# Cross-attention with LayerNorm: a new order for the last ten tiles, gamma and beta in two PSUM banks, late moments partly on ScalarE

## The chip, the cores and the metric

The kernel runs on one core of a Trainium2 chip. The core has five engines that run side by side, each through its own instructions in the order in which they were written: TensorE (PE: matrix products; PEld is its weight load), VectorE (DVE), ScalarE (ACT), GpSimd (POOL) and SyncE (SP, which only issues transfers). ACT and POOL issue transfers too. Matrix products are written to PSUM, eight banks of 128 partitions by 512 fp32 numbers; everything else lies in SBUF. The metric is the time of one execution on the device in microseconds (us); lower is better. A profile covers one execution; its span runs from the first instruction to the last.

## The reference

```python
qs = (q @ wq).reshape(Bq, Lq, H, HD).transpose(0, 2, 1, 3)
ks_ = (k @ wk).reshape(Bq, Lk, H, HD).transpose(0, 2, 1, 3)
vs = (v @ wv).reshape(Bq, Lk, H, HD).transpose(0, 2, 1, 3)
scores = jnp.einsum('bhqd,bhkd->bhqk', qs, ks_) / jnp.sqrt(jnp.float32(HD))
scores = jnp.where(mask[:, None, :, :], -jnp.inf, scores)
attn_w = jax.nn.softmax(scores, axis=-1)
attn = jnp.einsum('bhqk,bhkd->bhqd', attn_w, vs)
attn = attn.transpose(0, 2, 1, 3).reshape(Bq, Lq, H * HD)
out = attn @ wo + q
mu = jnp.mean(out, axis=-1, keepdims=True)
var = jnp.mean((out - mu) ** 2, axis=-1, keepdims=True)
return (out - mu) / jnp.sqrt(var + EPS) * gamma + beta
```

There are 4 batches of 2048 rows of 512 numbers (q), 77 context rows per batch (k and v), 16 heads of 32. In this kernel all is fp32 in and out.

## The kernel before

The 8192 rows are cut into 64 tiles of 128 rows (number t). Two tiles make a pair (b = t // 2). Products that must be exact to fp32 are made from a rounded high part and a low part: each costs three matmuls (high x high, high x low, low x high).

Tiles 0 to 53 are worked off in a loop (lines 600 to 704). For the last ten tiles, 54 to 63, and for the steps of earlier tiles that are still open, the order is written out by hand in the string `ORDER` (lines 45 to 65), and `do` (line 717) calls one step for each word. As each engine runs its instructions as they are written, a word's place settles what it queues behind. The words, by the engine that does them (the number is the tile, or the pair for P, V, a and b; what stands behind the point is a part):

- PE: `S` scores (line 285), four banks; `Q` a projection of queries (line 161); `V` weights x values of a pair (line 383), two banks; `W` the same for one tile, for pair 31 only (line 398), one bank; `O` output projection (line 447), 12 matmuls, one bank; `X` adds the residual on PE by two matmul records of the identity (line 436) ahead of `O`, so that the sum lies in PSUM.
- DVE: `T` masked maxima of four heads (line 299), which also empties a bank of the scores; `r`, `h` reciprocals of the sums (lines 324, 337); `t` transpose of a tile's weights (line 353); `b`, `d` low part of V's or W's product (line 418, written to `AL`); `+` residual for tiles without `X` (line 456); `s` moments by bn_stats and bn_aggr (lines 492 and 494); `y` centre: (out - mean) x gamma (line 518); `z` finish: x 1/std + beta (line 521); `q` copies a query projection.
- ACT: `e` exps of four heads with their sums (line 313); `a`, `c` high part of V's or W's product (line 414, written to `AH`); `k` scale by mean and 1/std (line 509); `K` scale by 1/std (line 512); `i` cast.
- POOL: `n`, `m` normalise the weights (whole tile, line 329; half a tile, line 343); `u` 1/std, two small instructions (lines 499 and 500); `v` the bias for `k`; `f` x gamma, then + beta (lines 483 and 484); `G` + beta (line 515); `j` low part of a cast.
- Transfers: `x` loads rows, `w` stores rows (SP); `P`, `U` move one of twelve parts of the transposed weights of a pair or a tile (line 365); the last letter names the queue: s SP, a ACT, g POOL. The transfer of a part starts when its `t` has run, and `V` or `W` needs all twelve.

So a late tile ends in one of three ways: `y` and `z` on DVE; `y`, `K`, `G`; or `k` and `f`. Row data lie in `od[t]`, in SBUF; while a tile's sum is still in PSUM it stands in `pos[t]`. All banks of PSUM come from one ring (`bank`, line 96): an allocation waits until the last reader of the bank eight allocations earlier is done. `gam` and `bet` are the rows of gamma and beta, spread over the partitions, in SBUF.

The last tiles end in the same order before and after the change: `W62`, `c62` (AH), `d62` (AL), `W63`, `X63`, `c63`, `d63`, `O62`, `O63`, then `s63`, `u63`, `y63`, `z63`, `w63`.

Of the kernel before, what the change touches and what calls it, by code (L numbers as in the profile page):

```python
# [42 lines left out]


ORDER = """
S54 T54.0 Q59 q58 T54.2 x57 i31 T54.3 S55 e54.0 j31 e54.2 T54.1 q59 x61 e54.1 e54.3 t53 T55.0 x52 O49 P26.2a r54
P26.5s T55.1 P26.6s k46 k47 e55.1 T55.2 +49 n54 S56 T55.3 s49 t54 T56.1 e55.2 Q62 q62 O48 T56.0 x56 f47 e55.0 S57
f46 T56.2 +48 e55.3 P26.9g e56.2 Q61 e56.0 r55 s48 T56.3 T57.2 T57.1 n55 T57.0 P26.7g V25 T57.3 S58 e56.3 e56.1 q61
u49 e57.0 P26.3s t55 a25.1 a25.0 P26.4s r56 P26.10s Q63 T58.3 e57.3 P26.8s P26.11s x60 b25.1 e57.2 P27.6g P26.0s w46
T58.0 T58.2 b25.0 q63 n56 x58 P26.1s P27.8s e57.1 P27.5s x62 P27.2g Q60 T58.1 P27.3g v49 e58.2 S59 P27.4g x51 t56  # L50
V26 O50 P27.11g r57 T59.0 P27.7s P27.9g P27.1g T59.2 n57 q60 P27.0g e58.0 P27.10s T59.3 T59.1 w47 t57 e58.1 a26.1
x50 a26.0 e58.3 b26.0 b26.1 e59.0 e59.2 P28.3g S60 P28.7g T60.1 P28.1g r58 u48 O51 T60.0 P28.8s T60.2 e59.1 +50
T60.3 +51 e59.3 n58 x53 t58 e60.3 r59 V27 S61 k49 P28.11s X52 s51 T61.0 T61.2 a27.0 P28.6g P28.10s O53 T61.3 n59 O52
P28.0s P28.2s x54 T61.1 x63 a27.1 e60.2 t59 P28.4g b27.1 e61.1 b27.0 y51 u51 P28.5g e61.2 e61.0 s50 e61.3 x55 f49
P29.2g e60.1 s52 P29.1g x59 S62 P28.9s P29.11s e60.0 T62.3 P29.0g y52 +53 r61 P29.9a T62.1 O55 T62.2 P29.6s T62.0
s53 e62.2 r60 +55 P29.3g u52 P29.5g n61 O54 t61 V28 K51 n60 S63 u53 a28.0 +54 e62.1 b28.0 t60 G51 P30.11g P29.4s
a28.1 P29.10s P29.8s b28.1 e62.0 T63.0 P29.7s P30.0g u50 e62.3 V29 a29.1 a29.0 y48 T63.1 v50 r62 X56 n62 s54 T63.3
w49 b29.1 P30.6g T63.2 b29.0 O57 P30.2s e63.1 P30.4s P30.5s k50 P30.10s t62 P30.9g f50 e63.0 e63.3 h63.0 U62.8g O56
P30.1s O59 y53 P30.8s P30.3s m63.0 e63.2 K53 X58 P30.7s U62.9g V30 U62.3s w50 +57 y54 U62.2s U62.1a U62.0a +59 a30.1
U62.10s s57 h63.1 m63.1 U62.5a s59 u54 O58 U62.4s s56 t63 a30.0 b30.0 K52 w51 U62.11a b30.1 X62 y57 u57 y56 U62.6s  # L60
U63.1g z48 U63.11s O60 G53 U63.7a U63.5g U63.6s O61 s55 U63.9s K54 U63.2g U62.7s U63.0a W62 U63.3s s58 z57 U63.8g
U63.4a +60 G54 c62 G52 U63.10s w53 y58 y59 u59 s60 w57 u56 w52 z59 +61 d62 u58 u60 w48 W63 s61 X63 w54 u55 K56 y55
w59 c63 z58 d63 y61 O62 G56 s62 y60 K55 u61 K60 w58 z61 w56 G55 O63 u62 G60 y62 w55 s63 z62 u63 w61 w60 y63 w62 z63
w63
"""


# [1 line left out]
def xattn_layernorm(  # L69
# [368 lines left out]
    def o_proj(t):  # L438
        b, tt = divmod(t, 2)
        rs = slice(tt * P, tt * P + P)  # L440
        ah, al = at[b]
        first = t not in pos
        if first:
            pos[t] = bank(f"po_{t}")
        for c in range(NC_D):
            for n, (a, w) in enumerate(((ah, woh), (ah, wol), (al, woh))):
                nc.tensor.matmul(  # L447
                    pos[t],
                    a[:, c, rs],
                    w[:, c, :],  # L450
                    start=(first and c == 0 and n == 0),
                    stop=(c == NC_D - 1 and n == 2),
                )

    def residual(t):
        nc.vector.tensor_tensor(od[t], pos.pop(t), od[t], ALU.add)  # L456
# [33 lines left out]
    def moments_one(t):  # L490
# [2 lines left out]
        mvs[t, 1] = sb.tile([P, 4], F32, tag="mvt", bufs=64 - LATE, name=f"mvt_{t}")  # L493
        nc.vector.bn_aggr(mvs[t, 1][:, :2], st)  # L494

    def rsqrt_one(t):
# [2 lines left out]
        nc.gpsimd.tensor_tensor(mv[:, 2:3], mv[:, 1:2], bat[t // TPB][1][:, k : k + 1], ALU.add)
        nc.gpsimd.tensor_tensor(mv[:, 2:3], mv[:, 2:3], mhalf[:, :1], ALU.pow)  # L500
# [10 lines left out]
    def stretch(t):
        nc.scalar.activation(od[t], od[t], AF.Identity, scale=mvs[t, 1][:, 2:3])

# [1 line left out]
        nc.gpsimd.tensor_tensor(od[t], od[t], bet, ALU.add)  # L515

    def centre(t):
        nc.vector.scalar_tensor_tensor(od[t], pos.pop(t, od[t]), mvs[t, 1][:, 0:1], gam, ALU.subtract, ALU.mult)  # L518

    def finish(t):  # L520
        nc.vector.scalar_tensor_tensor(od[t], od[t], mvs[t, 1][:, 2:3], bet, ALU.mult, ALU.add)  # L521
# [273 lines left out]
```

## Time and profile before

| what | us |
|---|---|
| median of 3 runs | 525.09 |
| lowest and highest | 524.68 and 526.96 |
| the profiled execution, its own time | 525.58 |
| its span | 523.8 |
| its time outside of the span | 1.78 |

Times in the rows that follow are counted from the start of the span. The first word of `ORDER`, `S54`, starts on PE at 423.44, so the part of the program that the change touches takes some 100 of the 523.8 us. A row of a timeline gives start, duration, engine, line, operation and shapes, and in square brackets how long the engine had been idle and what ended that. Matmuls overlap: their pace is the distance of two starts, not the duration.

### The profile page before, as it was taken

Reading aid. Unit: us, or ns where it says so; the run is one execution under the profiler, and the core shown is the slowest. Engines: PE = TensorE matmul, PEld = TensorE weight load, DVE = VectorE, ACT = ScalarE, POOL = GpSimd, SP = SyncE. Lnnn points to the kernel's source line nnn. Section 1 sums busy time; section 2 is a strip of 40 time slices with the busy share of each in tenths; the row PEclk is TensorE's granted clock in tenths of the full one; section 3 lists DMA queues with packets and bytes.
Section 4 is the critical chain, followed back from the end, with each engine's and each line's share of the span. In section 5 each row is a group of like instructions: output and inputs, shape, how many; then the busy total and the mean of one; then the engine's idle time right before and its main releaser. Section 6 shows DMA issues by size and latency. Waiting matters only on the chain. (4 is left out here: it accounts for less than half of the span.)

```text
span 523.8 us, 20456 instructions
## 1 busy us (share of the span) xinstructions
PE 511.1 (98%) x6852; PEld 388.8 (74%) x6852; DVE 482.7 (92%) x2584; ACT 467.2 (89%) x2224; POOL 419.8 (80%) x382
## 2 busy tenths in 40 slices
PE   9999999999999999999999999999999999999975
PEld 7977677777777777777777777777777777776653
DVE  5698899899999888999999889989999899999897
ACT  6688899999899999999899999999899999999511
POOL 0635457889799988898799988888989997888885
PEclk9999999999999999999999999999999999999997
DMA  8936667878777978787778788878877878894653
GB/s 309 402 127 163 181 157 200 225 219 239 183 189 211 237 203 229 220 225 197 195 209 233 214 227 215 221 195 225 209 198 209 232 215 191 220 251 133 182 187 140
DMA packets 58584, 110.24 MB, mean 210 GB/s; under 512 B 9392, under 2 KB 11056, under 8 KB 58480
## 3 DMA queue, kind: packets, MB, share of 16 engines
q1 hardware_dynamic: 55264, 102.44, 70.6%
q0 software_dynamic: 2496, 5.77, 4.0%
q8 instruction: 55, 0.90, 0.8%
q10 hardware_dynamic: 720, 0.72, 0.5%
q14 instruction: 49, 0.40, 0.3%
HBM read 41.79 MB, written 16.78 MB: 112 GB/s over the span
## 5 line engine op out<-in xcount | busy, mean ns | idle before, releaser
L313 ACT ACTIVATE pbuf<-pbuf,nm 128x77 f32<-128x77 f32 x1024 | 352.6, 353 | 22.5 <-DVE nm L299 16.6
L313 ACT ACTIVATION_READ_ACCUMULATOR pbuf<-pbuf,nm 128x1 f32 x1024 | 197.6, 193 | 0.0
L299 DVE CUSTOM_DVE_ANT_0 pbuf<-sc,mb 128x77 f32<-128x77 f32 x1024 | 170.5, 230 | 22.9 <-PE sc L285 22.9
L329 POOL TENSOR_TENSOR pbuf<-pbuf,ri 128x1232 f32<-128x1232 f32 x63 | 142.3, 2259 | 29.0 <-DVE ri L324 16.3
L447 PE MATMUL po<-woh,AH 128*128 128x512 f32 x256 | 108.1, 422 | 0.4 <-DVE AL L418 0.4
L447 PE MATMUL po<-woh,AL 128*128 128x512 f32 x256 | 101.4, 396 | 3.6 <-DVE AL L418 3.6
L447 PE MATMUL po<-wol,AH 128*128 128x512 f32 x256 | 101.1, 395 | 0.0
L161 PE MATMUL pq<-xth,wqh 128*128 128x512 f32 (+1 forms) x256 | 98.6, 385 | 0.9 <-DVE nm L299 0.9
L161 PE MATMUL pq<-xtl,wqh 128*128 128x512 f32 (+1 forms) x256 | 97.9, 382 | 0.0
L161 PE MATMUL pq<-xth,wql 128*128 128x512 f32 (+1 forms) x256 | 97.9, 382 | 0.0
L353 DVE STREAM_TRANSPOSE B<-pbuf 128x1280 f32<-128x1280 f32 x64 | 95.4, 1492 | 0.6 <-POOL pbuf L329 0.3
L299 DVE DVE_READ_ACCUMULATOR2_ANT nm<- 128x1 f32 x1024 | 83.2, 81 | 0.0
L483 POOL TENSOR_TENSOR o<-o,gam 128x512 f32<-128x512 f32 x50 | 66.2, 1325 | 13.6 <-ACT o L479 13.6
L285 PEld LDWEIGHTS sc<-kct,q 32*64 32x64 f32 x4096 | 51.3, 130 | 23.8 <-issue 22.8
L484 POOL TENSOR_TENSOR o<-o,bet 128x512 f32<-128x512 f32 x50 | 64.8, 1297 | 3.9
L154 POOL TENSOR_TENSOR xtl<-xtf,xth 128x1024 fp32r<-128x1024 f32 x28 | 67.2, 2401 | 0.0
L285 PE MATMUL sc<-kct,q 32*64 32x77 f32 x4096 | 61.3, 237 | 0.0
L383 PE MATMUL pa<-PT,vsb 96*32 96x256 f32 x992 | 60.0, 382 | 0.5 <-issue 0.3
L447 PEld LDWEIGHTS po<-woh,AH 128*128 128x128 f32 x256 | 48.7, 190 | 15.6 <-issue 1.3
L447 PEld LDWEIGHTS po<-woh,AL 128*128 128x128 f32 x256 | 48.7, 190 | 15.2 <-DVE AL L418 4.5
L161 PEld LDWEIGHTS pq<-xth,wqh 128*128 128x128 f32 x256 | 48.1, 188 | 10.8 <-PE sc L285 1.0
L447 PEld LDWEIGHTS po<-wol,AH 128*128 128x128 f32 x256 | 48.7, 190 | 9.1 <-issue 0.7
(113 smaller groups left out, 681.6 us busy)
## 6 DMA issues: line engine op xcount, KB each, us to landing
PT<-B SPq DMA_DIRECT2D x345, 128.0 KB
xtf<-xT SPq DMA_DIRECT2D x28, 512.0 KB
o<-x SPq DMA_DIRECT2D x56, 256.0 KB
out<-o SPq DMA_DIRECT2D x56, 256.0 KB
PT<-B POOLq DMA_DIRECT2D x25, 128.0 KB, 4.0
o_end<-x SPq DMA_DIRECT2D x8, 256.0 KB
out<-o_end SPq DMA_DIRECT2D x8, 256.0 KB
xtf<-xT SPq DMA_DIRECT2D x4, 256.0 KB
```

The costliest lines, as they stand in the source:

```text
L154: nc.gpsimd.tensor_tensor(l, fx.pop((g, c)), h.bitcast(F32), ALU.subtract)
L161: nc.tensor.matmul(pq, w[:, c, m * P : (m + 1) * P], r[:, c, rs], start=(n == 0), stop=(n == 11))
L285: nc.tensor.matmul(sc[j][half : half + P // 2, g * NK : (g + 1) * NK], qs[q, g, r0 : r0 + P // 2], kct[q, g, t // TPB, keys_of(j)], start= ...
L299: nc.vector.tensor_tensor_reduce(pb[:, h // 2, (h % 2) * NK : (h % 2 + 1) * NK], scs[t][j][:, g * NK : (g + 1) * NK], mb[:, t % TPB, keys_ ...
L313: nc.scalar.activation(pb[:, h // 2, (h % 2) * NK : (h % 2 + 1) * NK], pb[:, h // 2, (h % 2) * NK : (h % 2 + 1) * NK], AF.Exp, bias=nmax[t ...
L329: nc.gpsimd.tensor_tensor(pv, pv, rv.to_broadcast((P, NP, 2, NK)), ALU.mult)
L353: nc.vector.transpose(bt.rearrange("p c q r -> p q c r"), pbuf[t % NPB].rearrange("p q (c r) -> p q c r", c=5),)
L383: nc.tensor.matmul(pas[b, g // 2][HD * j : HD * (j + 1), (g % 2) * BLK : (g % 2 + 1) * BLK], vsb[:, 2 * b // TPB, HD * h : HD * (h + 1)], ...
L447: nc.tensor.matmul(pos[t], a[:, c, rs], w[:, c, :], start=(first and c == 0 and n == 0), stop=(c == NC_D - 1 and n == 2),)
L483: nc.gpsimd.tensor_tensor(o, o, gam, ALU.mult)
L484: nc.gpsimd.tensor_tensor(o, o, bet, ALU.add)
```

## The change

It has five parts.

1. `ORDER` is written anew (396 words for 397). The steps of attention are the same ones. For the ends of the tiles the counts change:

| word | before | after |
|---|---|---|
| s (DVE moments) | 16 | 11 |
| I, J (ACT mean, ACT squares; new) | 0 | 5 and 5 |
| y, z (DVE) | 14, 7 | 12, 12 |
| K (ACT), G (POOL) | 7, 7 | 0, 0 |
| k (ACT), v (POOL) | 4, 2 | 3, 1 |
| p (POOL scaling; new), f (POOL) | 0, 4 | 3, 6 |
| X (PE), + (DVE) | 5, 11 | 4, 12 |
| M (gamma, beta to PSUM; new) | 0 | 2 |
| P and U on SP, POOL, ACT | 44, 31, 9 | 55, 22, 7 |

2. `keep` (word `M`) copies gamma and beta with ACT into a bank each, which then leaves the ring. Seven banks go round behind `M0`, six behind `M1`.
3. `y` of a tile whose sum lies in SBUF takes gamma from its bank, and `z` takes beta from its bank. `y` of a tile whose sum lies in PSUM takes gamma from SBUF as before.
4. `I` and `J` make mean and sum of squares on ACT with its accumulator; `u` then divides by 512 in its first instruction. `p` subtracts the mean and scales on POOL; `f` follows it.
5. For tiles from 54 on, `O` makes the eight products with `AH` first and the four with `AL` last; before, they alternated (AH, AH, AL for each of four chunks).

```diff
+    ring, kept, rows, summed = [], set(), {}, set()
+
     def bank(name):
-        return ps.tile([P, 512], F32, tag="mm", name=name)
+        while len(ring) % 8 in kept:
+            ring.append(ring[-8])
+        ring.append(ring[-8] if kept else ps.tile([P, 512], F32, tag="mm", name=name))
+        return ring[-1]
+
+    def keep(k):
+        rows[k] = bank(f"row_{k}")
+        kept.add((len(ring) - 1) % 8)
+        nc.scalar.copy(rows[k], (gam, bet)[k])
...
-        for c in range(NC_D):
-            for n, (a, w) in enumerate(((ah, woh), (ah, wol), (al, woh))):
...
+        prods = [(n == 2, c, a, w) for c in range(NC_D) for n, (a, w) in enumerate(((ah, woh), (ah, wol), (al, woh)))]
+        if t >= 2 * CUT:
+            prods.sort(key=lambda p: p[0])
+        for n, (_, c, a, w) in enumerate(prods):
+            nc.tensor.matmul(pos[t], a[:, c, rs], w[:, c, :], start=(first and n == 0), stop=(n == 11))
...
+    def act_mean(t):
+        if "junk" not in ends:
+            ends["junk"] = sb.tile([P, NG, GRP], F32, tag="q", name="junk")
+        mvs[t, 1] = sb.tile([P, 4], F32, tag="mvt", bufs=64 - LATE, name=f"mvt_{t}")
+        nc.scalar.activation(
+            ends["junk"][:, t % NG], pos.get(t, od[t]), AF.Identity, scale=1.0 / D, accum_out=mvs[t, 1][:, 0:1]
+        )
+
+    def act_squares(t):
+        mv = mvs[t, 1]
+        nc.scalar.activation(
+            ends["junk"][:, t % NG], pos.get(t, od[t]), AF.Square, bias=mv[:, 0:1], scale=-1.0, accum_out=mv[:, 1:2]
+        )
+        summed.add(t)
...
+        if t in summed:
+            nc.gpsimd.tensor_scalar(mv[:, 2:3], mv[:, 1:2], 1.0 / D, eps, ALU.mult, ALU.add)
+        else:
+            nc.gpsimd.tensor_tensor(mv[:, 2:3], mv[:, 1:2], eps, ALU.add)
...
+    def pool_scale(t):
+        mv = mvs[t, 1]
+        nc.gpsimd.tensor_scalar(od[t], od[t], mv[:, 0:1], mv[:, 2:3], ALU.subtract, ALU.mult)
...
     def centre(t):
-        nc.vector.scalar_tensor_tensor(od[t], pos.pop(t, od[t]), mvs[t, 1][:, 0:1], gam, ALU.subtract, ALU.mult)
+        row = gam if t in pos else rows.get(0, gam)
+        nc.vector.scalar_tensor_tensor(od[t], pos.pop(t, od[t]), mvs[t, 1][:, 0:1], row, ALU.subtract, ALU.mult)
 
     def finish(t):
-        nc.vector.scalar_tensor_tensor(od[t], od[t], mvs[t, 1][:, 2:3], bet, ALU.mult, ALU.add)
+        nc.vector.scalar_tensor_tensor(od[t], od[t], mvs[t, 1][:, 2:3], rows.get(1, bet), ALU.mult, ALU.add)
```

The end of the order before (lines 58 to 64):

```
w49 b29.1 P30.6g T63.2 b29.0 O57 P30.2s e63.1 P30.4s P30.5s k50 P30.10s t62 P30.9g f50 e63.0 e63.3 h63.0 U62.8g O56
P30.1s O59 y53 P30.8s P30.3s m63.0 e63.2 K53 X58 P30.7s U62.9g V30 U62.3s w50 +57 y54 U62.2s U62.1a U62.0a +59 a30.1
U62.10s s57 h63.1 m63.1 U62.5a s59 u54 O58 U62.4s s56 t63 a30.0 b30.0 K52 w51 U62.11a b30.1 X62 y57 u57 y56 U62.6s
U63.1g z48 U63.11s O60 G53 U63.7a U63.5g U63.6s O61 s55 U63.9s K54 U63.2g U62.7s U63.0a W62 U63.3s s58 z57 U63.8g
U63.4a +60 G54 c62 G52 U63.10s w53 y58 y59 u59 s60 w57 u56 w52 z59 +61 d62 u58 u60 w48 W63 s61 X63 w54 u55 K56 y55
w59 c63 z58 d63 y61 O62 G56 s62 y60 K55 u61 K60 w58 z61 w56 G55 O63 u62 G60 y62 w55 s63 z62 u63 w61 w60 y63 w62 z63
w63
```

and after:

```
+54 P29.4s P29.10s P29.5s T63.3 p50 a28.0 b28.0 a28.1 P29.11s M0
r62 P29.1s x62 P30.3s e63.3 f50 s55 P30.2s P30.1s V29 P30.10s P30.7g n62 b28.1 y55 P30.9s a29.0 v51 a29.1 P30.5s X59
P30.6s b29.0 P30.4s s54 O56 I52 P30.11s P30.8s t62 e63.0 e63.1 y48 e63.2 P30.0g U62.7s u54 b29.1 k51 u55 h63.0 w50
O57 m63.0 +56 h63.1 I56 U62.9s U62.3s O59 U62.11s U62.6s U62.0g s53 y52 U62.8s U62.2s V30 m63.1 J52 M1 x63 a30.0 s59
t63 y59 U62.5a +57 U62.4a U63.9a J56 O58 y49 U63.3s U63.8s U63.10s z55 U62.1g b30.0 u49 a30.1 f51 X62 U63.2a U63.5s
b30.1 X61 U63.6s O60 u56 U63.1a y54 U63.0s z48 O61 w55 u53 U63.11s u52 z49 z54 U63.4a I57 y53 +58 U62.10a u59 p56
J57 I61 W62 z53 U63.7s f56 w51 +60 s58 u57 W63 z52 w48 u58 s60 z59 u60 X63 y60 w49 c62 w56 J61 y57 d62 w52 c63 d63
w59 w54 w53 z60 u61 O62 z57 w60 O63 p58 f58 y61 I62 z61 J62 w57 y62 u62 w58 s63 z62 w61 y63 u63 z63 w62 w63
```

More of the change, by code (lines that the diff above doesn't have):

```diff
@@ L45 @@
 ORDER = """
[L46 to L64, printed above, removed]
+i31 S54 Q59 T54.2 e54.2 x50 k46 T54.1 j31 T54.0 x56 q58 T54.3 S55 x59 O49 q59 e54.1 e54.3 T55.1 T55.0 T55.2 t53
+e54.0 e55.1 S56 r54 P26.7g Q61 x61 x58 k47 T55.3 e55.3 V25 P26.2s T56.3 n54 x51 T56.0 e55.0 +49 x57 P26.3s e55.2 f46
@@ new lines @@
+P26.4s T56.1 T56.2 q61 S57 a25.0 t54 r55 n55 T57.0 e56.1 P26.9s T57.1 b25.0 s49 P26.1g w46 Q63 T57.2 P26.0s O48
+a25.1 b25.1 S58 e56.0 t55 e56.3 P27.8s e56.2 Q62 T57.3 q63 P26.6g e57.2 Q60 P26.10g e57.0 f47 r56 P26.8s e57.1 T58.2
+P26.11s T58.3 T58.1 T58.0 P26.5g P27.1s x52 x60 +48 P27.7g e57.3 P27.3s e58.3 n56 P27.0g e58.1 S59 P27.10g q62 t56
+r57 s48 V26 q60 e58.2 T59.0 a26.1 T59.1 S60 e58.0 P27.2g T59.2 P27.11g O51 n57 t57 e59.2 T59.3 P27.5g a26.0 e59.3
+O50 T60.1 x53 P27.9s T60.3 r58 T60.0 +51 b26.1 e59.0 b26.0 P27.4s e59.1 T60.2 P27.6s e60.0 P28.6s P28.2g S61 P28.10s
@@ new lines @@
+u48 e60.2 P28.3s n58 t58 P28.1s +50 r59 T61.2 V27 T61.1 x54 P28.11s P28.7s T61.0 T61.3 O53 P28.4s e60.3 P28.8g n59
+t59 w47 S62 P28.0g a27.1 b27.1 O52 P29.6g e60.1 a27.0 T62.2 s51 b27.0 e61.0 e61.3 P28.5s e61.1 P29.8g P28.9s T62.1
+P29.2g r60 n60 O54 +53 T62.0 s50 S63 e61.2 T62.3 t60 e62.1 e62.3 P29.0g +52 u50 u51 x55 r61 T63.2 e62.0 O55 n61
+T63.0 P29.3s e62.2 +55 T63.1 P29.9s P29.7s t61 V28 +54 P29.4s P29.10s P29.5s T63.3 p50 a28.0 b28.0 a28.1 P29.11s M0
+r62 P29.1s x62 P30.3s e63.3 f50 s55 P30.2s P30.1s V29 P30.10s P30.7g n62 b28.1 y55 P30.9s a29.0 v51 a29.1 P30.5s X59
@@ L444, in o_proj @@
             pos[t] = bank(f"po_{t}")
-        for c in range(NC_D):
-            for n, (a, w) in enumerate(((ah, woh), (ah, wol), (al, woh))):
[L447 to L453, printed above, removed]
+        prods = [(n == 2, c, a, w) for c in range(NC_D) for n, (a, w) in enumerate(((ah, woh), (ah, wol), (al, woh)))]
[3 more added lines that the diff above has]
+            nc.tensor.matmul(pos[t], a[:, c, rs], w[:, c, :], start=(first and n == 0), stop=(n == 11))
     def residual(t):
@@ L498, in rsqrt_one @@
         k = t % TPB
-        nc.gpsimd.tensor_tensor(mv[:, 2:3], mv[:, 1:2], bat[t // TPB][1][:, k : k + 1], ALU.add)
+        eps = bat[t // TPB][1][:, k : k + 1]
+        if t in summed:
+            nc.gpsimd.tensor_scalar(mv[:, 2:3], mv[:, 1:2], 1.0 / D, eps, ALU.mult, ALU.add)
+        else:
+            nc.gpsimd.tensor_tensor(mv[:, 2:3], mv[:, 1:2], eps, ALU.add)
         nc.gpsimd.tensor_tensor(mv[:, 2:3], mv[:, 2:3], mhalf[:, :1], ALU.pow)
@@ L709, in xattn_layernorm @@
         "+": residual, "u": rsqrt_one, "y": centre, "z": finish, "k": scale, "f": affine, "w": store,
-        "v": bias_one, "K": stretch, "G": shift,
+        "v": bias_one, "K": stretch, "G": shift, "p": pool_scale, "I": act_mean, "J": act_squares, "M": keep,
     }
```

## The prediction

> **What bounds the kernel now.** I read the page first, then the busy times by stretches, then TensorE's timeline at the end, the chain of waits, and DVE, ACT and POOL around the last transpose.
>
> ```profile
> PE 511.1 (98%) x6852; PEld 388.8 (74%) x6852; DVE 482.7 (92%) x2584; ACT 467.2 (89%) x2224; POOL 419.8 (80%) x382
> ```
>
> ```profile
> 420.00:480.00 60.00, 59.51 (x974) 44.42 (x972) 59.15 (x361) 59.24 (x314) 51.11 (x57) 1.00 0.80 209
> 480.00:502.90 22.90, 22.03 (x118) 15.27 (x110) 21.41 (x60) 12.24 (x52) 19.85 (x27) 1.00 0.59 172
> ...
> 506.50:509.70 3.20, 0.02 (x2) 0.01 (x1) 3.17 (x7) 0.47 (x1) 1.69 (x5) 0.84 0.80 309
> 509.70:517.70 8.00, 8.00 (x22) 6.01 (x22) 7.57 (x11) 1.45 (x2) 6.39 (x8) 0.64 0.31 119
> ```
>
> Columns: stretch, length, busy time of PE, PEld, DVE, ACT, POOL, PE clock, share and rate of the transfers. From 420 to 480 PE, DVE and ACT are each busy for over 59 of 60 us: no single engine bounds there, and a new order can only shift waits. The end is another matter: PE stands still from 506.5 to 509.7 while DVE works, and then runs at a clock of 0.64.
>
> ```profile
> 502.98 2.01 PE L398 MATMUL pa<-PT,vsb 96*32 96x128 f32 x64
> 504.92 1.12 PE L436 MATMUL po<-o_end,ident 128*128 128x512 f32 x2
> 509.69 0.79 PE L447 MATMUL po<-woh,AL 128*128 128x512 f32 x1 [3.18 <-DVE AL L418]
> 510.28 0.63 PE L447 MATMUL po<-woh,AH 128*128 128x512 f32 x1
> ...
> 515.69 0.40 PE L447 MATMUL po<-wol,AH 128*128 128x512 f32 x1
> ...
> 517.31 0.40 PE L447 MATMUL po<-woh,AL 128*128 128x512 f32 x1
> ```
>
> `W62`, `W63` and `X63` are through at 506.0. `O62` makes two `AH` products and then waits 3.18 us for `d62` (AL). Behind that wait matmuls start 0.43 apart (510.28 to 515.40, twelve steps), later 0.23 apart (515.69 to 517.31, seven steps). So the wait costs itself and 13 x 0.20 = 2.6 us of slow clock. Why is `d62` late?
>
> ```profile
> 495.66 1.48 DVE B L353
> 497.14 1.17 DVE AL L418 x2
> 498.31 3.20 DVE o_end L518 x2
> 501.51 1.29 DVE o L521
> ...
> 505.06 0.60 DVE o_end L456
> 505.66 1.32 DVE o_end L518 x2
> ...
> 507.80 0.64 DVE o_end L521
> ...
> 509.04 0.61 DVE AL L418
> ...
> 517.75 0.71 DVE st L492
> ...
> 520.07 0.75 DVE o_end L521
> ```
>
> From `t63` (495.66) to `d62` (ends at 509.64) DVE works without a pause; `d62` is simply far back in its queue. In that stretch two `y` take 3.20 where two later ones take 1.32, and a `z` takes 1.29 where another takes 0.64.
>
> **The price of two rows from SBUF.**
>
> ```profile
> L518 DVE SCALAR_TENSOR_TENSOR o<-o,mvt,gam 128x512 f32<-128x512 f32 x5 | 5.9, 1186 | 0.0
> L518 DVE SCALAR_TENSOR_TENSOR o_end<-o_end,mvt,gam 128x512 f32<-128x512 f32 x4 | 5.8, 1442 | 0.0
> L518 DVE SCALAR_TENSOR_TENSOR o_end<-po,mvt,gam 128x512 f32<-128x512 f32 x4 | 3.0, 742 | 0.0
> L521 DVE SCALAR_TENSOR_TENSOR o_end<-o_end,mvt,bet 128x512 f32<-128x512 f32 x6 | 4.4, 732 | 0.1
> ```
>
> Nine `y` with both operands in SBUF take 11.7 us, where the form with one operand in PSUM takes 0.742 each: an excess of 11.7 - 6.7 = 5.0, or 0.56 each. Six of the seven `z` pay nothing (0.732). The change puts one operand of all twelve `z` and of the eight `y` from SBUF into PSUM. PSUM as the second operand has no row; PSUM as the first has one, and I take its price, 0.66 from start to start. Bounds: no excess, or all of 0.56 left.
>
> [...]
>
> **Step 1: `t63` starts earlier, 495.66 to 491.1.**
>
> ```profile
> 468.51 1.71 DVE L518 SCALAR_TENSOR_TENSOR o<-o,mvt,gam 128x512 f32<-128x512 f32 x1
> ...
> 488.52 0.98 DVE L518 SCALAR_TENSOR_TENSOR o<-o,mvt,gam 128x512 f32<-128x512 f32 x1
> ...
> 490.02 1.17 DVE L518 SCALAR_TENSOR_TENSOR o<-o,mvt,gam 128x512 f32<-128x512 f32 x1
> ...
> 493.97 0.20 DVE L337 RECIPROCAL ri<-sum 128x8 f32<-128x8 f32 x1 [1.35 <-ACT pbuf L313]
> ```
>
> ```profile
> 488.09 0.18 ACT L313 ACTIVATION_READ_ACCUMULATOR pbuf<-pbuf,nm 128x1 f32 x1
> 492.45 0.36 ACT L313 ACTIVATE pbuf<-pbuf,nm 128x77 f32<-128x77 f32 x1 [4.18 <-POOL pbuf L343]
> ```
>
> DVE: ahead of `t63` the new order has two `s` and two `y` fewer (2 x 0.79 + 2 x 0.66 = 2.9). The excess of `y51`, `y53` and `y54` (0.96, 0.23, 0.42 over 0.75) and the idle 1.35 go: 5.9 in all, so DVE could start at 489.8. ACT: `e63.2` stands behind `m63.0` today and waits 4.18 for it; in the new order it stands ahead of it. Ahead of its end ACT has one more quarter of exps (1.4), `M0` (0.6) and `I52` (0.9), but two `k` (1.6), `K51` (0.7) and two transfers (1.2) fewer: 0.6 less, so `e63.2` ends 0.6 ahead of where the queue stands today at 488.27, at 487.7. POOL then:
>
> ```profile
> 494.32 1.22 POOL L343 TENSOR_TENSOR pbuf<-pbuf,ri 128x616 f32<-128x616 f32 x1 [1.40 <-DVE ri L337]
> 495.51 0.18 POOL L499 TENSOR_TENSOR mvt<-mvt,nz 128x1 f32<-128x1 f32 x1
> 495.77 0.56 POOL L500 TENSOR_TENSOR mvt<-mvt,small 128x1 f32<-128x1 f32 x1
> ```
>
> `m63.0`, `U62.0g` and `m63.1` take 1.22 + 0.6 + 1.22 and end at 490.7 at the earliest. I take 491.1 for `t63`. Bounds: 489.8 by DVE's queue alone; 495.7 if waits elsewhere give all of it back.
>
> **Step 2: `d62`, 509.64 to 506.2.** Behind `t63` DVE has six `y`, seven `z`, three `+`, two `b`, two `s` and `d62`: 1.43 + 6 x 0.66 + 7 x 0.65 + 3 x 0.60 + 1.17 + 2 x 0.79 + 0.60 = 15.1, so it ends at 506.2. That is more work than today (13.98, of which 2.5 was excess): `z` for `K` and `G` is no gift to DVE, which gains by the start.
>
> **Step 3: PE.** Up to `X63` the same matmuls stand in nearly the same order, one `X` less (0.55): `O62` starts at 505.4. It has eight `AH` products first, which last to 505.4 + 8 x 0.23 = 507.2; `d62` at 506.2 is in time by 1.0. There is no wait and no slow clock: 24 x 0.23 + 0.15 = 5.7, so `O63` ends at 511.1 instead of 517.7. Both covers are needed: with today's alternation PE would idle from 505.9 to 506.2. What comes next in lateness is `W62`, which needs `U62.10a`, issued by ACT:
>
> ```profile
> L414 ACT CAST AH<-pa 128x512 fp32r<-128x512 f32 x64 | 34.0, 578 | 7.3 <-PE pa L398 5.6 <-PE pa L383 1.6
> L512 ACT ACTIVATE o<-o,mvt 128x512 f32<-128x512 f32 x5 | 3.6, 717 | 6.4 <-POOL mvt L499 4.8 <-DVE AL L418 1.5
> ```
>
> ```profile
> L365 ACTq DMA_DIRECT2D PT<-B x7: 592/615/834, 493.0 to 498.7; - x7
> DMA to landing us min/median/max: 2.1/2.2/4.1
> ```
>
> `I` and `J` have no row. The nearest is `K` on the same tile, 0.72, with 0.18 for reading the accumulator: 0.9. Bounds: 0.7, and 2.0 if a sum over 512 numbers costs more than the rows show. Behind `e63.2` (487.7) ACT does `k51`, `I56`, `J52` and `M1`, meets `V30`'s end at about 492.1 for `a30.0`, then issues three transfers, and does `J56`, `a30.1`, three more transfers and `I57`: 0.6 + 1.9 + 0.9 + 0.6 + 1.9 + 0.9 = 6.8, so `U62.10a` is out at 499.5 and lands between 501.7 and 503.6. PE wants `W62` at 502.4. A late landing costs up to 1.2, all of it on PE. I charge nothing, because 502.4 keeps the idle time that PE has today (0.5 in the first stretch, 0.9 in the second), and put the 1.2 into the range.
>
> **Step 4: the end.** At 511.1 DVE has done `d63`, `z60`, `z57`, `y61`, `z61` and `y62` (506.2 + 3.9 = 510.1). From `O63`'s last matmul to the end of `z63` today's 517.73 to 520.82 stays, 3.1, and from there to the span's end 3.0: 517.2. With 1.78 outside of the span that is 519.0, 6.6 less than the profiled 525.58. The median of the runs is 0.5 below that execution; I don't take it off.
>
> POOL is covered: from 490.7 it has `U62.1g`, eight `u` (0.8 each), `p56`, `p58` and `f51`, `f56`, `f58`:
>
> ```profile
> L483 POOL TENSOR_TENSOR o<-o,gam 128x512 f32<-128x512 f32 x50 | 66.2, 1325 | 13.6 <-ACT o L479 13.6
> ```
>
> Three `f` at 2 x 1.3, two `p` at the same row's 1.3, 8 x 0.8 and 0.6 give 17.4, to 508.1. `u63` is wanted at 512.0. `p` has no row: 0.6 or 2.6 (two operations) are its bounds, and the upper one puts the end of `f58` at 510.7 (two `p` ahead of it), still in time. The eleven transfers more on SP run 0.6 each in a queue that today waits for its producers; they cost nothing, unless they come late for `V30`.
>
> **Rivals.**
>
> *A: the waits come back earlier.* `S60` and `S63` get their banks from maxima written one and two words ahead (14 ahead for `S63` today), and seven, then six banks go round. If each of five such places costs PE one quarter of maxima (0.63) or a little more, 4 us are lost of the 6.6: 523.0. For it: PE, DVE and ACT all have under 1 us of slack in 60. Against it: the same stretch runs without waits today in an order just as dense.
>
> *B: the banks don't free DVE, and the kernel is slower.* If `y` and `z` from SBUF keep an excess of 0.56, `d62` comes 15 x 0.56 = 8.4 later, at 514.6; PE stops for 7.4, the slow clock is back, 16 matmuls take 13 x 0.43 + 3 x 0.23 = 6.3 and `O63` ends at 521.1; with 1.1 for the last two `z` the end is at 521.1 + 3.1 + 1.1 + 3.0 + 1.78 = 530.0. It decides from about 0.45 on; at 0.36 it is 526.6. For it: there are 15 such operations ahead of `d62`, where few pay today. Against it: the four rows at 742 ns.
>
> *C: the moments on ACT cost 2.0.* Then `e63.2` is 1.1 late and `U62.10a` 5.5, `W62` starts near 508, PE has idled 6 us, and `W`, `X` and `O` run at the slow clock: 3.5 + 24 x 0.23 + 13 x 0.20 + 0.15 = 11.8, to 519.8 and 527.7. Against it: an exp over 77 with its sum costs 0.35 from start to start.
>
> **How the numbers follow.** A change within 0.5% (2.6 us: 522.5 to 527.7) can't be told from none. Forecast 0.66, with a range of its own of 516.5 to 522; A 0.14, a third of it below 522.5; B 0.10, mostly slower; C 0.10, a third of it within. Faster: 0.65 + 0.05 = 0.70. Within: 0.01 + 0.09 + 0.02 + 0.03 = 0.15. Slower: 0.08 + 0.07 = 0.15. The low end is 519.0 less PE's idle 1.4 and less 0.9, by which the lowest run shown lies below the profiled execution, rounded down: 516.0. The high end stops short of C and B, at 527.5; 0.04 and 0.15 are left out.
>
> **What would show it.** Right: `y` and `z` at 0.7 throughout; `t63` near 491; no wait ahead of `AL` in `O62`, and steps of 0.23 to the end; the last matmul near 511. Wrong: a PE wait of over 2 us between 440 and 500 (A), rows of `z` above 1.0 us (B), `W62` waiting for a transfer (C).

## The result, and the profile after

| | before | after |
|---|---|---|
| median of the runs, us | 525.31 (524.68 to 526.96) | 519.55 (519.02 to 519.57) |
| the profiled execution, its own time | 525.58 | 519.53 |
| its span | 523.8 | 517.7 |

The ratio is 0.9883, with a 95% interval from 0.9859 to 0.9907. The times before are the three shown above and one more that stood beside the new kernel. In the code of after, `y` is L547, `z` L550, `O` L458, `t` L362, `b` and `d` L427, `s` L497 and L499, `u` L521 (after `J`) or L523, then L524, `I` L505, `J` L511, `p` L537, `f` L488 and L489.

The busy times of the page, and then the same stretches as before (length; busy time of PE, PEld, DVE, ACT, POOL; PE clock; share and rate of the transfers):

```profile
PE 506.8 (98%) x6850; PEld 386.4 (75%) x6850; DVE 475.4 (92%) x2578; ACT 469.7 (91%) x2238; POOL 413.6 (80%) x371
```

```profile
420.00:480.00 60.00, 58.89 (x970) 44.38 (x968) 57.52 (x379) 59.12 (x319) 47.18 (x47) 1.00 0.76 199
480.00:502.90 22.90, 22.90 (x170) 16.86 (x166) 22.01 (x47) 14.72 (x54) 20.98 (x30) 1.00 0.72 208
...
506.50:509.70 3.20, 3.09 (x14) 2.56 (x15) 3.10 (x6) 1.47 (x4) 3.12 (x3) 1.00 0.72 277
509.70:517.70 8.00, 0.83 (x4) 0.37 (x2) 3.91 (x7) 0.00 (x0) 3.31 (x6) 0.68 0.38 147
```

Up to 480 nothing is won: PE even idles 1.11 of 60 us there, for 0.49 before. From 480 to 502.9 PE has no gap left (0.87 before). The stretch from 506.5 to 509.7, in which PE stood still, is now full of matmuls at the full clock, and behind 510.5 PE has nothing to do, where it worked for 8 us at a clock of 0.64 before. So most of the gain lies in the last 15 us. TensorE's timeline there:

```profile
501.48 1.95 PE L407 MATMUL pa<-PT,vsb 96*32 96x128 f32 x64
...
503.93 0.80 PE L458 MATMUL sc<-woh,AH 128*128 128x512 f32 x1
...
506.61 1.19 PE L458 MATMUL sc<-woh,AL 128*128 128x512 f32 x4 [0.27 <-DVE AL L427]
507.64 0.40 PE L458 MATMUL sc<-woh,AH 128*128 128x512 f32 x1
...
509.46 1.07 PE L458 MATMUL sc<-woh,AL 128*128 128x512 f32 x4
```

`W62` starts 1.50 earlier (502.98 before), the wait for `d62` is 0.27 instead of 3.18, and the matmuls keep their pace (eight steps of 0.23 from 507.64 to 509.46), so that the 2.6 of slow clock are gone: 1.5 + 2.9 + 2.6 = 7.0. Not all of the 1.50 is the change's: `S54` already starts 0.44 earlier (423.00 for 423.44), 0.55 is the `X` that there is less, and PE's idle time in the two first stretches is 0.25 less (1.11 for 1.36). The last product starts at 509.46 + 3 x 0.23 = 510.15 instead of 517.31, 7.2 earlier. But the time fell by only 6.05. DVE and POOL at the end show where 1.1 went:

```profile
491.33 1.51 DVE L362 STREAM_TRANSPOSE B<-pbuf 128x1280 f32<-128x1280 f32 x1 [0.30 <-POOL pbuf L352]
...
505.87 1.28 DVE L427 TENSOR_TENSOR AL<-pa,AH 128x512 fp32r<-128x512 f32 x2
...
510.57 0.70 DVE L497 BATCH_NORM_STATS2 st<-sc 128x6 f32<-128x512 f32 x1
...
512.50 0.75 DVE L550 SCALAR_TENSOR_TENSOR o_end<-o_end,mvt,sc 128x512 f32<-128x512 f32 x1 [1.01 <-POOL mvt L524]
...
514.01 0.75 DVE L550 SCALAR_TENSOR_TENSOR o_end<-o_end,mvt,sc 128x512 f32<-128x512 f32 x1
```

```profile
506.77 2.08 POOL L537 TENSOR_SCALAR o_end<-o_end,mvt 128x512 f32<-128x512 f32 x1
508.94 1.30 POOL L488 TENSOR_TENSOR o_end<-o_end,gam 128x512 f32<-128x512 f32 x1
510.31 1.26 POOL L489 TENSOR_TENSOR o_end<-o_end,bet 128x512 f32<-128x512 f32 x1
511.56 0.26 POOL L521 TENSOR_SCALAR mvt<-mvt,nz 128x1 f32<-128x1 f32 x1
511.90 0.56 POOL L524 TENSOR_TENSOR mvt<-mvt,small 128x1 f32<-128x1 f32 x1
```

`s63` starts 7.18 earlier (517.75 before). Behind it stands `z62`, which needs `u62`; POOL comes to `u62` only after `p58` and `f58`, and is done at 512.46. DVE idles 1.01 for it. So `z63` ends at 514.76, 6.06 before the 520.82 of before, which is the whole gain of the profiled execution. The groups from 420 on, by form (busy us, mean ns of one, idle ahead of them):

```profile
L547 DVE SCALAR_TENSOR_TENSOR o<-o,mvt,row 128x512 f32<-128x512 f32 x6 | 4.4, 729 | 0.0
L550 DVE SCALAR_TENSOR_TENSOR o_end<-o_end,mvt,sc 128x512 f32<-128x512 f32 x6 | 4.4, 741 | 1.2 <-POOL mvt L524 1.0
L550 DVE SCALAR_TENSOR_TENSOR o<-o,mvt,sc 128x512 f32<-128x512 f32 x6 | 4.3, 739 | 0.0
...
L547 DVE SCALAR_TENSOR_TENSOR o_end<-o_end,mvt,row 128x512 f32<-128x512 f32 x2 | 1.4, 742 | 0.0
...
L511 ACT ACTIVATE junk<-o_end,mvt 128x512 f32<-128x512 f32 x2 | 1.4, 724 | 1.4 <-DVE o_end L547 1.4
...
L505 ACT ACTIVATE junk<-o_end 128x512 f32<-128x512 f32 x2 | 1.3, 632 | 2.7 <-DVE AL L427 2.4 <-DVE o_end L461 0.3
```

All `y` and `z` with one operand in PSUM take 0.71 to 0.75 each (0.729 to 0.742 in the mean of each group above); none pays an excess. `I` takes 0.63 and `J` 0.72 from SBUF (0.60 and 0.69 from PSUM), each with some 0.19 for reading the accumulator. `p` takes 2.08.

### The profile page after: what moved, and what is told of

Same layout as the page of the kernel before. It is cut to its first block, busy times and chain, and to the rows that moved or that the text cites. A ratio compares the mean times of both kernels' runs of the same rounds, so it can differ in the third digit from the quotient of the medians.

```text
span 517.7 us, 20457 instructions
## 1 busy us (share of the span) xinstructions
PE 506.8 (98%) x6850; PEld 386.4 (75%) x6850; DVE 475.4 (92%) x2578; ACT 469.7 (91%) x2238; POOL 413.6 (80%) x371
## 4 chain that ended last, share of the span: by engine, by line
PE 86%; POOL 4%; DVE 4%; DMA 2%; SPq 2%; issue 1%; ACT 0%; POOLq 0%; DVEq 0%
PE pq L170 31%; PE po L458 31%; PE sc L294 11%; PE pa L392 10%; PE pv L231 2%; PE pk L196 1%; SPq L374 1%; DMA stage_a<-wk 1%; DVE B L362 1%; POOL mvt L524 1%; DVE pbuf L308 1%; POOL o_end L537 1%; DMA o<-x 1%; POOL o_end L488 1%; POOL o_end L489 0%
## 5 line engine op out<-in xcount | busy, mean ns | idle before, releaser
L362 DVE STREAM_TRANSPOSE B<-pbuf 128x1280 f32<-128x1280 f32 x64 | 95.5, 1494 | 2.3 <-DMA o<-x 1.6
L458 PE MATMUL po<-woh,AH 128*128 128x512 f32 x232 | 96.8, 417 | 0.0
L458 PE MATMUL po<-wol,AH 128*128 128x512 f32 x232 | 90.6, 391 | 0.0
L458 PE MATMUL po<-woh,AL 128*128 128x512 f32 x232 | 88.6, 390 | 0.0
L308 DVE DVE_READ_ACCUMULATOR2_ANT nm<- 128x1 f32 x1024 | 84.8, 83 | 0.0
L488 POOL TENSOR_TENSOR o<-o,gam 128x512 f32<-128x512 f32 x50 | 66.2, 1324 | 13.9 <-ACT o L484 13.8
L489 POOL TENSOR_TENSOR o<-o,bet 128x512 f32<-128x512 f32 x50 | 64.4, 1288 | 3.9
L392 PE MATMUL pa<-PT,vsb 96*32 96x256 f32 x960 | 58.0, 382 | 0.6 <-DMA o_end<-x 0.3
L170 PEld LDWEIGHTS pq<-xth,wql 128*128 128x128 f32 x256 | 48.1, 188 | 9.4
L170 PEld LDWEIGHTS pq<-xtl,wqh 128*128 128x128 f32 x256 | 48.1, 188 | 9.2
L458 PEld LDWEIGHTS po<-woh,AH 128*128 128x128 f32 x232 | 43.5, 187 | 12.5 <-issue 0.7
```

What stands on the lines that cost most here:

```text
L170: nc.tensor.matmul(pq, w[:, c, m * P : (m + 1) * P], r[:, c, rs], start=(n == 0), stop=(n == 11))
L308: nc.vector.tensor_tensor_reduce(pb[:, h // 2, (h % 2) * NK : (h % 2 + 1) * NK], scs[t][j][:, g * NK : (g + 1) * NK], mb[:, t % TPB, keys_ ...
L362: nc.vector.transpose(bt.rearrange("p c q r -> p q c r"), pbuf[t % NPB].rearrange("p q (c r) -> p q c r", c=5),)
L392: nc.tensor.matmul(pas[b, g // 2][HD * j : HD * (j + 1), (g % 2) * BLK : (g % 2 + 1) * BLK], vsb[:, 2 * b // TPB, HD * h : HD * (h + 1)], ...
L458: nc.tensor.matmul(pos[t], a[:, c, rs], w[:, c, :], start=(first and n == 0), stop=(n == 11))
L488: nc.gpsimd.tensor_tensor(o, o, gam, ALU.mult)
```

## The experiments

The theory behind them: the time is set by how late `d62` is against `O62`'s first `AL` product. The banks, the moments on ACT and the earlier `e63.2` bring `d62` forward; the order of the products hides what is left. The main rivals: the gain comes from the new order of the words alone, and the banks cost as much as they bring, because fewer banks go round. Each median below is to be seen beside 525.12 of the kernel before on the same chip, or 525.43 for the two runs that move `y56` and for the last one under "POOL's wait at the end"; ratios are against it. Single rows of two traces differ without a cause, too: `S54`, ahead of every change, starts at 423.44 before and at 423.00 after, and `t63` at 491.00, 491.33 and 491.43 in three traces of kernels that differ only in the products or behind `t63`.

### The banks, taken away in the new order

The rows of gamma and beta are read from SBUF, while the two banks stay out of the ring:

```diff
-        row = gam if t in pos else rows.get(0, gam)
+        row = gam
...
-        nc.vector.scalar_tensor_tensor(od[t], od[t], mvs[t, 1][:, 2:3], rows.get(1, bet), ALU.mult, ALU.add)
+        nc.vector.scalar_tensor_tensor(od[t], od[t], mvs[t, 1][:, 2:3], bet, ALU.mult, ALU.add)
```

> The changed kernel, with both banks still kept but y and z reading gamma and beta from SBUF again. Theory (two SBUF operands make a DVE operation wait for GpSimd, and DVE's queue up to d62 sets the end): an excess of 0.36 to 0.56 us on each of the 15 such operations ahead of d62, d62 5 to 8 us later, PE stands still for over 3 us ahead of the AL products of O62, slow clock behind it; 526 to 530 us. Rival (the new order alone brings the gain, the banks are idle talk): y and z stay near 0.73 us, within 1 us of 519.5.

525.61 us, ratio 1.0009 [0.9992, 1.0026]: without the reads from PSUM nothing of the gain is left. The rival falls. The time is a little under the theory's 526 to 530. The groups of `y` and `z` in this run:

```profile
L547 DVE SCALAR_TENSOR_TENSOR o<-o,mvt,gam 128x512 f32<-128x512 f32 x6 | 7.5, 1253 | 0.0
L550 DVE SCALAR_TENSOR_TENSOR o<-o,mvt,bet 128x512 f32<-128x512 f32 x6 | 4.8, 829 | 0.0
L550 DVE SCALAR_TENSOR_TENSOR o_end<-o_end,mvt,bet 128x512 f32<-128x512 f32 x6 | 4.6, 785 | 1.9 <-POOL mvt L524 1.7
...
L547 DVE SCALAR_TENSOR_TENSOR o_end<-o_end,mvt,gam 128x512 f32<-128x512 f32 x2 | 1.4, 742 | 0.0
```

The twenty take 18.3 us; in the changed kernel they take 4.4 + 4.4 + 4.3 + 1.4 = 14.5. The excess is 3.8, or 0.19 each, where 0.36 to 0.56 was expected. And it isn't spread over them. DVE's timeline and POOL's beside it:

```profile
482.85 2.79 DVE L547 SCALAR_TENSOR_TENSOR o<-o,mvt,gam 128x512 f32<-128x512 f32 x1
...
493.53 1.51 DVE L362 STREAM_TRANSPOSE B<-pbuf 128x1280 f32<-128x1280 f32 x1 [0.30 <-POOL pbuf L352]
...
496.20 1.82 DVE L547 SCALAR_TENSOR_TENSOR o<-o,mvt,gam 128x512 f32<-128x512 f32 x1
...
503.72 0.74 DVE L550 SCALAR_TENSOR_TENSOR o<-o,mvt,bet 128x512 f32<-128x512 f32 x1
```

```profile
482.81 2.27 POOL L338 TENSOR_TENSOR pbuf<-pbuf,ri 128x1232 f32<-128x1232 f32 x1
...
496.20 1.26 POOL L489 TENSOR_TENSOR o<-o,bet 128x512 f32<-128x512 f32 x1
497.46 0.69 POOL L521 TENSOR_SCALAR mvt<-mvt,nz 128x1 f32<-128x1 f32 x1
...
502.95 2.20 POOL L537 TENSOR_SCALAR o_end<-o_end,mvt 128x512 f32<-128x512 f32 x1
```

The `y` at 482.85 meets a normalisation that POOL began 0.04 earlier, and ends at 485.64, 0.56 after POOL; the one at 496.20 ends at 498.02, 0.56 after POOL's addition. These two pay 2.05 + 1.08 of the 3.8. A `z` that runs within POOL's `p`, which reads one SBUF tensor, pays nothing (0.74). So in this run the price is a wait for a whole two-operand instruction of POOL, and falls only on those that meet one. `t63` starts 2.20 later and `d62` 4.1 later. On PE that is this:

```profile
510.75 1.72 PE L458 MATMUL sc<-woh,AL 128*128 128x512 f32 x4 [2.55 <-DVE AL L427]
512.26 0.63 PE L458 MATMUL sc<-woh,AH 128*128 128x512 f32 x1
512.68 0.63 PE L458 MATMUL sc<-wol,AH 128*128 128x512 f32 x1
```

Behind the wait of 2.55 the slow clock is back (steps of 0.42 to 0.43 from 512.26 to 514.39, a granted clock of 0.53 from 511 to 514), and with it the 6 us. A delay of 4 on DVE became 6 of time: `s63` starts 5.7 later (516.28), and `z62` waits 0.4 longer for `u62` (1.39).

In a second version `M0` and `M1` are left out as well, so that all eight banks go round:

> As after_sbuf_rows, but without the copies M0 and M1, so eight banks go round to the end. Theory: no wait in the changed kernel comes from the smaller ring, so this one equals after_sbuf_rows within 0.7 us (two copies of 0.6 us on ACT less, and M0's wait of 0.9 us). Rival (six banks cost PE time that the change pays for its rows): over 1.5 us faster than after_sbuf_rows.

525.91 us, ratio 1.0020 [1.0006, 1.0034], as without the reads alone. So two banks less in the ring cost nothing in this version, whose end hangs on DVE as well (`O62` waits 2.55 here, too). For the changed kernel itself there is only its trace: between 440 and 500 no wait of PE is over 0.32.

### Gamma's bank alone, in the old order

The kernel before, with `keep`, the shorter ring and `centre` as changed, `M0` written behind `e63.3`, and the old order of the products; beta stays in SBUF.

> The old kernel with one edit: gamma is copied to a bank behind e63.3 (where ACT is idle) and y of tiles in SBUF takes it from there; beta stays in SBUF, order and products as before. Theory: y53, y54, y57, y55 and y61 lose their excess of 0.2 to 1.9 us, 4.1 in all; d62 comes 2.5 us earlier, PE waits about 1.2 instead of 3.18 us ahead of AL, no slow clock; 521 us (520.5 to 522). Rival (what is gained on DVE is eaten by waits on POOL or PE): 524 to 525.5.

523.05 us, ratio 0.9958 [0.9941, 0.9974], between the two. The `y` that took 2.62 before, at 498.23, under POOL's `G`, takes 0.72 at the same place:

```profile
498.38 0.72 DVE L548 SCALAR_TENSOR_TENSOR o_end<-o_end,mvt,row 128x512 f32<-128x512 f32 x1
```

```profile
498.22 1.28 POOL L544 TENSOR_TENSOR o<-o,bet 128x512 f32<-128x512 f32 x1
```

```profile
499.91 0.47 PE L459 MATMUL po<-woh,AH 128*128 128x512 f32 x1 [2.58 <-DVE o_end L548]
```

But with seven banks the old order makes `O60` wait 2.58 for `y56` to give its bank back, and the slow clock follows (mean 0.67 from 499.9 to 505). The bank's price, which the changed kernel's trace doesn't show, is paid here. To take it away, `y56` is written right behind `t63`:

```diff
-s56 t63 a30.0 b30.0 K52 w51 U62.11a b30.1 X62 y57 u57 y56 U62.6s
+s56 t63 y56 a30.0 b30.0 K52 w51 U62.11a b30.1 X62 y57 u57 U62.6s
```

> The old order and the old order of products with only gamma's bank, as in the run that came to 523.05, but with y56 written right behind t63, ahead of a30.0 and b30.0. There O60 had waited 2.58 for y56 to give its bank back, and 2.4 were lost behind that to the slow clock. Theory: y56 ends at about 498.0, O60 waits some 0.7 for the bank and 0.6 for b30.0 and starts without a slow clock, so W62 runs at about 504 (507.15 before). d62 stands behind the same work on DVE less its idle 0.8 and so ends at about 509, O62 waits at its third product for some 2 to 3 us, and the time is 521 to 522.5. Rival: what the bank's wait took was hidden behind DVE's queue anyway, and the time stays within 0.4 of 523.05.

522.51 us, ratio 0.9939 [0.9924, 0.9954]. PE is as expected up to `W62` (`O60` waits 0.77, `W62` starts at 503.60), but the time is just above the theory's upper end and little below the rival's. The reason is not the one that was given: `O62` waits only 0.71 for `d62`, and PE's last product starts at 513.55. DVE, without a pause, comes to `s63` only at 514.63. Its queue sets the end, with two `z` among it (1.34 and 1.61) that still read beta from SBUF. The intervals of this run and the one without the move overlap, so a gain of the move isn't shown by the times.

```profile
514.63 0.69 DVE L498 BATCH_NORM_STATS2 st<-sc 128x6 f32<-128x512 f32 x1
```

The same with the new order of the products:

> The same kernel with the new order of the products from tile 54 on (eight with AH first, then the four with AL). Theory: O62's eight AH products cover 1.4 us of the wait for d62, no slow clock follows, and the two covers together are worth more than either alone (the bank alone is bounded by d62, the products alone were worth nothing): 0.8 to 2 us below the kernel without them, at 520 to 521. Rival: as in the old kernel with these products alone, DVE is busy without a pause up to the last y, so that no more than 0.4 comes of it.

522.58 us, ratio 0.9946 [0.9929, 0.9962]: no gain, and the rival is right. `O62` waits no more, its last products start at 511.59, and DVE comes to `s63` at 514.39.

### The order of the products

In the old kernel alone (the `prods` lines of the change, nothing else):

> The old kernel with one edit: O of tiles from 54 on makes its eight AH products first. Theory (PE and DVE tie at the end of the old kernel: DVE works without a pause from 495.7 to 517.3): O62 waits 2.1 us instead of 3.18 ahead of AL, the clock stays up, O63 ends near 514 instead of 517.7, but s63 has to wait for y62 on DVE until 517.3, so only 0.4 us come of it: 524.5 to 525.1 us. Rival (the wait of 3.18 us and the slow clock behind it are the loss): 521 to 522.

525.07 us, ratio 0.9998 [0.9988, 1.0008]. The wait fell from 3.18 to 2.17. The expected "clock stays up" failed: behind the four `AL` products the matmuls start 0.43 apart, and the granted clock from 511 to 514 is 0.50 (the last row, in the columns of the stretches).

```profile
509.65 1.20 PE L449 MATMUL po<-woh,AL 128*128 128x512 f32 x4 [2.17 <-DVE AL L418]
...
511.05 0.63 PE L449 MATMUL po<-wol,AH 128*128 128x512 f32 x1
511.48 0.63 PE L449 MATMUL po<-woh,AH 128*128 128x512 f32 x1
```

```profile
511.00:514.00 3.00, 3.00 (x8) 2.34 (x7) 3.00 (x4) 0.72 (x1) 2.91 (x4) 0.50 0.27 105
```

PE is through at 515.2 all the same, 2.5 earlier than before (517.7), and nothing is won, since DVE has work without a pause up to `y62` and reaches `s63` at 517.24 (517.75 before).

In the changed kernel, with the old alternation (`if t >= 2 * CUT` becomes `if False`):

> The changed kernel with the products of O alternating AH, AH, AL as before. Theory: d62 now comes at 506.5, so O62 waits 2 us behind its first two products where it had waited 0.27; that is under the 3.18 us that slowed the clock, so O63 ends 1.4 us later and, since z62 waits for POOL until 512.5 anyway, the end moves by 0.5 to 1.0 us: 520 to 520.7. Rival (the new order of the products is what keeps the clock up): steps of 0.43 us again and 522 to 524.

519.33 us, ratio 0.9894 [0.9879, 0.9909]: not slower at all, against the expectation. PE and DVE:

```profile
506.27 0.50 PE L458 MATMUL sc<-woh,AL 128*128 128x512 f32 x1 [1.65 <-DVE AL L427]
```

```profile
511.59 0.70 DVE L497 BATCH_NORM_STATS2 st<-sc 128x6 f32<-128x512 f32 x1 [0.43 <-PE sc L458]
...
512.42 0.71 DVE L550 SCALAR_TENSOR_TENSOR o_end<-o_end,mvt,sc 128x512 f32<-128x512 f32 x1
```

PE does wait 1.65, and `s63` comes 1.02 later; but `z62` runs at 512.42, as in the changed kernel (512.50), where it waits for POOL. The two delays lie side by side.

### POOL's wait at the end

`p56` and `p58`, 2.08 each on POOL, become `v` (POOL, two small instructions) and `k` (ACT, idle at both places):

```diff
-U62.10a u59 p56
+U62.10a u59 v56 k56
...
-w60 O63 p58 f58 y61
+w60 O63 v58 k58 f58 y61
```

> The changed kernel with p56 and p58 (2.08 us each on POOL) replaced by v and k (0.4 us on POOL, 0.8 on ACT, which is idle there). Theory: z62 waited 1.01 us for u62, which stood behind p58 and f58 on POOL; with 1.7 us less on POOL that wait goes and z62 follows s63 at once; 518.5 us (518.2 to 518.9). Rival (the wait is for J62 on ACT or for the end of O62, and POOL's queue is only named last): no change, 519.5.

518.66 us (518.07 to 518.94), ratio 0.9870 [0.9852, 0.9889]. It is the lowest of all kernels, below each of the four runs of the changed one; the intervals of the two ratios overlap, so it is the trace that shows the cause. DVE's end:

```profile
510.65 0.70 DVE L497 BATCH_NORM_STATS2 st<-sc 128x6 f32<-128x512 f32 x1
...
511.49 0.72 DVE L550 SCALAR_TENSOR_TENSOR o_end<-o_end,mvt,sc 128x512 f32<-128x512 f32 x1
...
512.97 0.75 DVE L550 SCALAR_TENSOR_TENSOR o_end<-o_end,mvt,sc 128x512 f32<-128x512 f32 x1
```

`z62` follows `s63` without a pause, and `z63` ends 1.04 earlier, at 513.72.

If POOL's wait hid the order of the products, the old alternation must cost something in this kernel:

> The kernel that came to 518.66 (the changed kernel with its two last scalings on ACT, so that POOL's u62 is no longer waited for), with the old alternation of the products. Theory: now the end hangs on O63 and s63 alone, O62 waits about 1.6 us for its first AL product, O63 ends about 1.0 later, and the time is 519.4 to 519.8, 0.8 to 1.1 more. Rival: DVE's queue up to y62 sets the end anyway, and the time stays within 0.3 of 518.66.

520.08 us, ratio 0.9895 [0.9881, 0.9910]: 1.4 more, a little above the theory's 0.8 to 1.1, and 1.1 where each is set against the kernel before beside it (525.43 and 525.12). `O62` waits 1.60, `s63` starts at 512.08 (510.65 without the alternation), and nothing hides it now. So the order of the products is worth 1.1 to 1.4, but only where neither POOL nor DVE is later than PE.

### The moments and `e63.2`

The five `I` and `J` go back to bn_stats on DVE (`I52` becomes `s52`, `J56` becomes `s56`, and likewise for 57, 61 and 62; the other halves of the pairs are dropped):

> The changed kernel with the moments of tiles 52, 56, 57, 61 and 62 on DVE again (bn_stats, bn_aggr) in place of the squares on ACT. Theory: five times 0.79 us on DVE, 3.0 of it ahead of d62, which comes at 509.4; PE waits 3.0 us ahead of the AL products of O62; DVE is through with y62 at 514.5, so the end moves by 3 us with the clock up and by 5 with it down: 522.5 to 524.5. Rival (DVE has room, the moments could have stayed): within 1 us of 519.5.

523.19 us, ratio 0.9967 [0.9949, 0.9985], as expected.

```profile
509.77 2.07 PE L458 MATMUL sc<-woh,AL 128*128 128x512 f32 x4 [3.21 <-DVE AL L427]
```

`d62` comes 3.2 later, PE stands for 3.21 and runs at the slow clock behind it (0.73 from 508 to 511 and 0.70 from 511 to 514).

`e63.2` goes back behind `m63.0`, as it was in the old order:

```diff
-t62 e63.0 e63.1 y48 e63.2 P30.0g U62.7s u54 b29.1 k51 u55 h63.0 w50
-O57 m63.0 +56 h63.1
+t62 e63.0 e63.1 y48 P30.0g U62.7s u54 b29.1 k51 u55 h63.0 w50
+O57 m63.0 e63.2 +56 h63.1
```

> The changed kernel with e63.2 behind m63.0 again, as in the old order. Theory of the prediction (the start of t63 moved since e63.2 no longer waits for m63.0): if the wait itself is the cause, t63 starts 3 us or more later and 2 to 4 us are lost. Rival (POOL was late with m63.0 in the old kernel because f50 and transfers stood ahead of it, and in the new one it isn't): e63.2 waits about 1 us, t63 starts 0.5 to 1.0 us later, 519.5 to 520.3.

520.67 us, ratio 0.9911 [0.9893, 0.9929], 1.1 more and between the two. ACT and PE:

```profile
489.83 0.36 ACT L322 ACTIVATE pbuf<-pbuf,nm 128x77 f32<-128x77 f32 x1 [2.36 <-POOL pbuf L352]
```

```profile
508.93 1.19 PE L458 MATMUL sc<-woh,AL 128*128 128x512 f32 x4 [0.81 <-DVE AL L427]
```

The wait of ACT is real and `t63` starts 2.36 later (493.69), but PE starts `O62` later too (505.71) and waits only 0.81, and no slow clock follows (1.00 from 508 to 514). Part of PE's delay is, by an estimate, a wait for a bank: `y59`, the last reader of the bank that `X62` gets, ends at 495.81 (493.48 in the changed kernel), and `O61` starts 1.78 later (500.45 for 498.67), which puts `X62`, 4.48 ahead of `O61` in the changed kernel, at 495.97. `s63` is 2.32 later than in the changed kernel (512.89), `z62` then waits 0.38 for `u62` instead of 1.01, and `z63` ends 1.69 later; this execution, at 521.19, is the slowest of its four, whose median is 1.1 above the changed kernel's.

## Why the prediction was right, and where it was not

The time was forecast at 519.0 and came to 519.55, by the path that was forecast. By its steps:

**What bounds the kernel.** Right in that DVE's queue up to `d62` had to become shorter: the wait for `d62` and the slow clock behind it are gone, and PE's idle time shows nothing won before 480. But the wait and the 2.6 of slow clock were not to be had by themselves: with the new products alone PE was through 2.5 earlier and the time stayed (525.07), as DVE came to `s63` only 0.5 earlier.

**The price of two rows from SBUF.** The reading is right, and it carries the whole gain: with SBUF rows the new order is worth nothing (1.0009). That the excess goes with the second operand in PSUM was the author's estimate, from a form with the first one there; the changed kernel shows it. The value taken for an operand in PSUM, 0.66 from start to start, holds: the instructions take 0.729 to 0.742 with the row in PSUM, and 0.742 for two `y` from SBUF beside which POOL runs only small instructions. Mis-sized was the excess as a price of each: 0.56 was a mean over instructions that paid nothing and such that waited for all of a POOL instruction. In the new order it was 0.19. So rival B, 15 x 0.56 = 8.4 and 530.0, was too dear even for a kernel without the banks: that one came to 525.6.

**Step 1.** `t63` at 491.33 for 491.1, and `e63.2` ends at 487.77 for 487.7. The two runs that take one part away put `t63` 2.2 later without the reads from PSUM and 2.4 later with `e63.2` behind `m63.0`.

**Step 2.** `d62` ends at about 506.5 (half of the pair that starts at 505.87) for 506.2, 15.2 behind `t63` for 15.1.

**Step 3.** Two terms were off. `O62` starts at 503.93 for 505.4. Of the 1.5, 0.55 is a misreading: the forecast took the end of `X63`'s row for the start of `O62`, which lies 0.55 ahead of it (505.48 before). 0.44 was there at `S54` already, and 0.25 is idle time of PE that the forecast kept (1.11 for 1.36); the rest isn't traced. `I` and `J` cost 0.75 (497.23 to 497.98) and 0.72 (490.30 to 491.02) from start to start, for 0.9. So "`d62` is in time by 1.0" failed: PE waits 0.27. And "both covers are needed" was not borne out: alternating products alone lose nothing in the changed kernel (519.33), as POOL is as late. That sentence looked at PE alone; 1.1 to 1.4 is what the order of the products brings once POOL is out of the way.

**Step 4.** This is the step that failed: "POOL is covered", with `u63` as the first that is wanted. `p` cost 2.08 for 1.3, within its bounds, yet `f58` ends at 511.57, behind the 510.7 of the upper bound: ahead of it stand nine `u`, not eight (0.8), and POOL is through with `m63.1` at 491.3, not 490.7. And behind `f58` stands `u62` ahead of `u63`, and `z62` wants it at 511.5. POOL has it at 512.46. It costs 1.0, and the run with `k` in place of `p` gets that back. Against the forecast, PE ends 0.6 early, the wait then gives 1.1 back, and the sum is 0.5 too low: two errors of opposite sign, each larger than what is left. That they nearly cancel is luck.

**Rivals A and C.** No wait of PE between 440 and 500 is over 0.32, so A is out in the changed kernel. It isn't far off: with `e63.2` back behind `m63.0` a bank is, by the estimate above, waited for once, and in the old order with seven banks it was real, with 2.58 at one place. C is out: `I` and `J` cost 0.63 and 0.72, not 2.0.

**What the parts are worth.** Taken away one by one, the reads from PSUM are worth 6.1, the moments on ACT 3.6, `e63.2` 1.1 and the products nothing. They don't add up to 5.8 and needn't: some of the lateness of `d62` is hidden by `z62`'s wait for POOL (1.01), and behind PE waits of 2.55 and 3.21 the slow clock adds to it. The old order with gamma's bank and room for its ring had 2.9 of the gain; the rest needs DVE relieved as well. How much of it beta's bank would bring in that order wasn't tried.

## What to carry to other kernels

Look at what runs on GpSimd beside a VectorE instruction with two SBUF operands: a mean duration hides that some wait for the whole of a GpSimd instruction (the mean of 1.253 in the run with SBUF rows is that of one at 2.79, one at 1.82 and four at 0.71 to 0.74), and a row that is read often can be kept in PSUM if the ring of banks can spare one (0.71 to 0.75 for each `y` and `z` that reads it there in the changed kernel). When a long wait of TensorE is shortened, find at once which queue is next in lateness: here DVE up to `y62`, PE, and POOL up to `f58` all end within some 1 us (510.5 to 511.6), and a part that is worth 1.1 to 1.4 by itself shows nothing behind another. For each engine that is to be "covered", check the first result that is wanted from its queue, not the last.
